# Layer 0's neighbour sum as seven products of half blocks in a two-layer graph kernel

## The chip, the cores and the metric

The program runs on one core of one Trainium2 chip. The metric is the device time of one execution in microseconds. Before the change it is 1271.28 us, the median of three runs (1270.83 to 1271.75).

## What is computed

There are 16 graphs (a "batch" b below is one graph) of 1024 nodes with 256 features. Two layers follow each other, each with a residual and a layer norm. Cut to what matters:

```python
# layer 0 (adj is 0 or 1 in the data, symmetric, with ones on the diagonal)
e0    = leaky(einsum('bid,bjd->bij', h * a0[:, 0], h))       # leaky: x or 0.2 x
alpha = sigmoid(where(adj == 1, e0, -max))
x     = layernorm(x + einsum('bij,bjd->bid', alpha, x) + bias)
# layer 1
Hh    = einsum('bni,io->bno', x, W)
s, d  = Hh @ a[:256], Hh @ a[256:]
e     = where(adj != 0, exp(-leaky(s[:, :, None] + d[:, None, :])), 0)
x     = layernorm(x + elu(einsum('bnm,bmo->bno', e, Hh) / e.sum(-1)))
```

All of it is fp32. A second, general pass for adjacency values other than 0 and 1 stands behind a flag and does not run with these inputs.

## The kernel before, in words

A batch has 1024 rows, eight tiles of 128. Everything is unrolled; the order of each engine's instructions is the order in which the code emits them (a manual schedule), and a scheduler adds the semaphores. An instruction that waits holds up all that stands behind it on its engine or queue. One turn of the loop over b (L572) has three stages and mixes three batches: layer 0 of b, layer 1 of b - 1 (`prev`) and the output of b - 2 (`done`).

**Strips** (L580 to L601). The matrix alpha is symmetric but for the mask, so only its upper triangle is computed. `strip(b, jt)` (L219) multiplies row tile jt with all columns from jt on: TensorE makes chunks of at most 512 columns in `ps_e` (three PSUM buffers), ACT takes two tanh of each (L241, L242), DVE their maximum (L243). `finish` (L245) adds one and multiplies by the adjacency (L249, DVE), and POOL adds twice the identity on the diagonal block (L259), which is the residual: `als[b]` is twice what multiplies x. `dump` (L261) turns 32 x 32 blocks on DVE (L265) and writes them to DRAM, `gather` (L271) fetches them as the mirrored blocks below the diagonal, both on SP's DMA queue; `mask(b, t)` (L277, L280, DVE) applies the adjacency to column tile t below the diagonal. In between, `project(prev, t)` (L397) multiplies the normed rows of b - 1, features on partitions in `x1T`, with W and the two vectors (TensorE, L411), and ACT takes exponentials (L419 to L421). `share_p` (L423) spreads one of the vectors over all partitions through DRAM on POOL's queue.

**Layer 0's sum** (L608 to L626). For each of eight row tiles t, `sum0` (L337) multiplies all eight blocks of column t with x: 8 x 8 products of 128 x 128 by 256 columns, each a pair of MATMUL records (L348), into a PSUM bank of `ps_acc` (three buffers). `end0` (L356) halves and adds the bias (L358, DVE, from PSUM) and takes the norm's statistics (`stats`, L299); after four tiles POOL computes the inverse roots (`center`, L321) and ACT scales the rows (`scale0`, L331). Beside this DVE does masks 3 to 6 and `weights(prev, m)` (L454, L460), ACT the scaling of b - 2's output and `check_adj` (L124). The normed rows go to DRAM (`save_x1`, L372) and come back in 32 x 32 blocks (`fetch_x1`, L380), which DVE turns (`turn_x1`, L385, L387): that is `x1T` for the next turn's projections.

**Layer 1's sum** (L631 to L671). For each row tile `sum1` (L464, L465) multiplies eight blocks of e with 257 columns; `elu` (L473) and `add` (L500) follow on DVE and ACT. Here x of b + 1, loaded in blocks, is turned and scaled (`turn_x`, L193: DVE, then ACT into `xa`), which the next strips need. SP carries `load_x`, `load_blocks` and the stores of the output; POOL's queue carries the adjacency (`load_adj`, L96, int32 to bf16).

Batch 0 has a start of its own (L525 to L570), the last batch an end of its own.

Of the kernel before, what the change touches and what calls it, by code (L numbers as in the profile page):

```python
# [18 lines left out]
P = 128  # L19
# [11 lines left out]
def one_kind_pass(  # L31
# [57 lines left out]
    def load_x(b, queues):  # L89
        xs[b] = two.tile([P, NT, D], F32, tag="x", name=f"x_{b}")  # L90
        rows = x[b].rearrange("(t p) d -> p t d", p=P)
        n = NT // len(queues)
        for g, queue in enumerate(queues):
            queue.dma_start(xs[b][:, ts(g, n), :], rows[:, ts(g, n), :])
# [43 lines left out]
    arow = two.tile([P, D], F32, tag="h", name="arow")[0:ND, 0:P]  # L138
    nc.scalar.dma_start(arow, a0.rearrange("(c p) o -> c (p o)", p=P))
# [23 lines left out]
    load_x(1, [nc.gpsimd])  # L163
# [4 lines left out]
    pcol = ps_e.tile([P, HALF], F32, tag="e", name="pcol")[:, 0:ND]  # L168
    nc.tensor.transpose(pcol, arow, ident[0:ND, 0:ND])
    nc.scalar.copy(acol, pcol)  # L170
# [5 lines left out]
    def make_Wx(c):  # L176

        for s in range(2):
            wprod = two.tile([P, D], F32, tag="h", name=f"wprod_{c}_{s}")
            nc.vector.tensor_tensor(wprod, Wx[:, c, 2:], a_bc[:, ts(s, D)], ALU.mult)  # L180
            nc.vector.tensor_reduce(Wx[:, c, s : s + 1], wprod, AX.X, ALU.add)

# [123 lines left out]
    def rstd(mv, what):  # L306
# [3 lines left out]
        nc.gpsimd.tensor_scalar(ve, mv[:, :, 1], EPS, None, ALU.add)  # L310
# [10 lines left out]
    def center(mv, what):  # L321

        r = rstd(mv, what)
# [3 lines left out]
        nc.gpsimd.tensor_scalar(mr, mr, -1.0, None, ALU.mult)  # L327
        return [(r[:, t : t + 1], mr[:, t : t + 1]) for t in range(n)]
# [4 lines left out]
    x1s, mv0s, r0s = {}, {}, {}  # L333
# [3 lines left out]
    def sum0(b, t):  # L337
        multiply0(b, t)
        end0(b, t)

    def multiply0(b, t):
        if t == 0:
            x1s[b] = two.tile([P, NT, D], F32, tag="x1", name=f"x1_{b}")
            mv0s[b] = small.tile([P, NT, 2], F32, tag="mv0", name=f"mv0_{b}")
            r0s[b] = []
# [10 lines left out]
    def end0(b, t):  # L356
        y = x1s[b][:, t, :]
        nc.vector.scalar_tensor_tensor(y, accs[t], 0.5, bias_bc, ALU.mult, ALU.add)  # L358
        stats(y, mv0s[b][:, t, :], f"0_{b}_{t}")
        if t % HT == HT - 1:  # L360
            g = t // HT
            r0s[b] += center(mv0s[b][:, ts(g, HT), :], f"0_{b}_{g}")
# [3 lines left out]


    x1Ts, Hs, pqs, p_bcs, es = {}, {}, {}, {}, {}

    x1_rows = {}  # L370
# [26 lines left out]
    def project(b, t):  # L397
# [21 lines left out]
        nc.scalar.activation(w, pt[:, 1:2], AF.Exp, scale=-SLOPE)  # L419
        nc.scalar.activation(pqs[b][:, :, t], pt[:, 0:2], AF.Exp, scale=SLOPE - 1.0)  # L420
        nc.scalar.mul(Hs[b][t][:, 0:D], pt[:, 2:], w)  # L421
# [108 lines left out]
    nc.sync.dma_start(bias_bc, bias.partition_broadcast(P))  # L530

# [12 lines left out]
    for t in range(NT):  # L544
# [12 lines left out]
        if t < 2:  # L557
            make_Wx(t)
        if t == 1:
# [4 lines left out]
        if t in (4, 5):  # L564
            scale0(0, 2 * t - 8)
            scale0(0, 2 * t - 7)
            turn_x(1, t - 4)
        if t == 5:
            save_x1(0, 0)
            fetch_x1(0, 0)  # L570

    for b in range(1, B):  # L572
# [4 lines left out]
        if prev == 0:  # L577

            projects = [[], [], [0, 1], [2, 3], [4, 5], [6, 7], [], []]
        for jt in range(NT):  # L580
            if jt == 4:
                mask(b, 0)
            strip(b, jt)
            if prev == 0 and jt < 2:
                scale0(0, HT + 2 * jt)
                scale0(0, HT + 2 * jt + 1)
# [5 lines left out]
            if prev == 0 and jt == 2:  # L592
                transpose_x1(0)
            if jt >= 1:
                gather(b, jt - 1)
            for t in projects[jt]:
                project(prev, t)
            if jt == 6:
                share_p(prev)
            if jt >= 6:  # L600
                mask(b, jt - 5)  # L601
        check_pq(prev)
        if not last:
            load_x(b + 1, [nc.sync])
# [3 lines left out]
        for t in range(NT):  # L608
            if 1 <= t < 5:
                mask(b, t + 2)  # L610
            for m in ([], [], [0, 1], [2], [3], [4], [5], [6, 7])[t]:
                weights(prev, m)
            if done >= 0:
                scale1(done, t)
                if t in (3, 7):
                    store(done, t - 3, HT)
            sum0(b, t)
            if t == 5 and not last:
                load_adj(b + 1, 0)
            if t in (5, 6):  # L620
                scale0(b, 2 * t - 10)
                scale0(b, 2 * t - 9)
            if t == 6:
                save_x1(b, 0)
            if t >= NT - CHECKS:
                check_adj(b, t - NT + CHECKS)  # L626
        if not last:
            load_adj(b + 1, 1)


        for t in range(NT):  # L631
# [3 lines left out]
            if last and t == 6:  # L635
                turn_x1(b, 1)
            if last and t == 3:
                turn_x1(b, 0)
# [9 lines left out]
            if t == 0:  # L648
                fetch_x1(b, 0)
            if t in (1, 2):  # L650
                scale0(b, 2 * t + 2)
                scale0(b, 2 * t + 3)
            if t == 2:
                save_x1(b, 1)
            if t == 4:
                fetch_x1(b, 1)
                if not last:
                    turn_x1(b, 0)
            if not last and t in (3, 5):
                turn_x(b + 1, (t - 3) // 2)  # L660
            if not last and t == 6:
                turn_x1(b, 1)
            if last and t in (4, 6):
# [3 lines left out]
                share_half(b, t0)  # L667
        if not last:
# [522 lines left out]
```

## Time and profile before

| what | value |
|---|---|
| median of three runs | 1271.28 us |
| span of the profiled execution, first to last instruction | 1268.6 us |
| around it (median less span) | 2.7 us |
| mean granted TensorE clock | 0.999 |
| L348, layer 0's products, 128x256 | 2048 records, 445.5 us busy |
| L465, layer 1's products, 128x257 | 2032 records, 444.9 us busy |
| DVE busy, all of the span | 925.2 us |
| DMA | 180.77 MB, 142 GB/s on average |

The execution time of the profiled run is not listed beside its span, so the median of the runs stands for it. PE is TensorE (matmul records), PEld its weight loads, DVE the vector engine, ACT the scalar engine, POOL GpSimd, SP the engine that issues most DMAs. In a group's line, "acc<-x,al" names what is written and read, xN the number of instructions, then the busy time, the mean in ns of one instruction, and the idle time ahead of them with what ended it. The mean of a matmul counts its time in the pipeline; what it costs in a row of others is read from the chain or from sums of busy time. In the timeline the first two columns are the start and the duration in us.

### The profile page before, as it was taken

The page shows a single profiled execution, that of the slowest core. Times are in us where ns is not written, and L with a number is a line of the kernel's source. Part 1 is how long each engine was busy: PE and PEld are TensorE (multiplying, and loading weights), DVE is VectorE, ACT ScalarE, POOL GpSimd, SP SyncE. Part 2 cuts the span into 40 slices and gives each one's busy share as a digit, 9 for nine tenths or more (in the row PEclk, how much of TensorE's full clock was granted, in tenths as well). Part 3 has the DMA queues.
Part 4 walks back from the last instruction along what each step waited for, and adds up shares of the span by engine and source line. Part 5 has one row for each costly group of instructions (what it writes and reads, how often), then busy time and mean ns, then how long its engine had stood idle before and what let it go on. Part 6 is the DMA issues. An engine that isn't in the chain of part 4 may idle for free.

```text
span 1268.6 us, 17528 instructions
## 1 busy us (share of the span) xinstructions
PE 1259.2 (99%) x5476; PEld 1024.5 (81%) x5476; DVE 925.2 (73%) x2027; ACT 650.2 (51%) x1467; POOL 299.7 (24%) x605
## 2 busy tenths in 40 slices
PE   9999999999999999999999999999999999999997
PEld 7788787887878878788787887878778787887886
DVE  5686867868678686876868868687686877858657
ACT  4645645456353564545645445454455644456434
POOL 2212231212312122121222212223122231212213
PEclk9999999999999999999999999999999999999999
DMA  9489595795959869497694966949579595895422
GB/s 213 80 171 155 92 197 92 168 185 106 190 90 177 168 124 198 78 174 159 131 203 83 184 131 139 210 80 190 113 167 185 97 192 95 171 183 99 109 51 69
DMA packets 603832, 180.77 MB, mean 142 GB/s; under 512 B 482010, under 2 KB 585940, under 8 KB 603732
## 3 DMA queue, kind: packets, MB, share of 16 engines
q1 hardware_dynamic: 581760, 135.85, 54.4%
q0 software_dynamic: 21280, 43.06, 18.7%
q8 instruction: 46, 0.75, 0.3%
q10 hardware_dynamic: 692, 0.66, 0.1%
q14 instruction: 54, 0.44, 0.1%
HBM read 152.44 MB, written 60.62 MB: 168 GB/s over the span
## 4 chain that ended last, share of the span: by engine, by line
PE 98%; DVE 1%; ACT 0%; issue 0%; ACTq 0%; DVEq 0%
PE acc L348 35%; PE acc L465 34%; PE pe L233 20%; PE pH L411 9%; PE busy L146 0%; PE pal L288 0%; PE pxT L209 0%; DVE st L301 0%; DVE y L505 0%; DVE y L503 0%; PE prow L427 0%; ACT y L331 0%; ACT y_kept L331 0%; ACT L680 0%; DVE mv L303 0%
## 5 line engine op out<-in xcount | busy, mean ns | idle before, releaser
L348 PE MATMUL acc<-x,al 128*128 128x256 f32 x2048 | 445.5, 379 | 0.0
L465 PE MATMUL acc<-H,e 128*128 128x257 f32 x2032 | 444.9, 379 | 0.0
L465 PEld LDWEIGHTS acc<-H,e 128*128 128x128 f32 x2032 | 384.9, 189 | 56.9
L348 PEld LDWEIGHTS acc<-x,al 128*128 128x128 f32 x2048 | 387.5, 190 | 51.8
L233 PE MATMUL pe<-xa,xT 128*128 128x384 f32 (+1 forms) x720 | 251.0, 486 | 0.0
L233 PEld LDWEIGHTS pe<-xa,xT 128*128 128x128 f32 x720 | 132.7, 189 | 80.9 <-issue 42.6
L331 ACT ACTIVATE x<-x,mr,r 128x256 f32<-128x256 f32 x128 | 69.4, 592 | 227.2 <-POOL mr L327 227.2
L460 DVE SCALAR_TENSOR_TENSOR e<-p,pq_kept,adj 128x1024 f32<-128x1024 f32 (+1 forms) x136 | 160.8, 1208 | 25.4 <-DMA p<-p_row 25.4
L310 POOL TENSOR_SCALAR ve<-mv 128x4 f32<-128x4 f32 (+2 forms) x49 | 16.2, 332 | 622.8 <-DVE mv L303 616.2
L497 ACT ACTIVATE h<-acc,rinv 128x256 f32<-128x256 f32 x126 | 59.1, 469 | 200.5 <-DVE rinv L489 185.1
L241 ACT ACTIVATE tb<-pe 128x512 f32<-128x512 f32 (+1 forms) x192 | 94.1, 490 | 120.3 <-PE pe L233 91.1
L488 DVE TENSOR_SCALAR rinv<-acc 128x1 f32<-128x1 f32 x127 | 19.9, 157 | 157.3 <-PE acc L465 156.8
L243 DVE TENSOR_TENSOR tb<-tb,low 128x512 f32<-128x512 f32 (+1 forms) x192 | 103.4, 544 | 38.6 <-ACT low L242 38.3
L128 ACT ACTIVATE junk<-adj,minus 128x2048 bf16<-128x2048 bf16 x64 | 127.3, 1989 | 0.0
L411 PE MATMUL pH<-Wx,x1T 128*128 128x258 f32 x512 | 126.3, 381 | 0.0
L411 PEld LDWEIGHTS pH<-Wx,x1T 128*128 128x128 f32 x512 | 97.2, 190 | 35.8 <-issue 14.3
L259 POOL TENSOR_TENSOR al<-ident,al 128x128 f32<-128x128 f32 x128 | 66.6, 520 | 227.2 <-DVE al L249 226.7
L249 DVE SCALAR_TENSOR_TENSOR al<-tb,adj 128x512 f32<-128x512 f32 (+7 forms) x132 | 97.5, 739 | 5.3 <-DVE tb L243 0.4
L242 ACT ACTIVATE low<-pe 128x512 f32<-128x512 f32 (+1 forms) x192 | 93.2, 485 | 0.5 <-DVE tb L243 0.5
L280 DVE SCALAR_TENSOR_TENSOR al<-al,adj 128x512 f32<-128x512 f32 (+3 forms) x150 | 76.1, 531 | 21.8 <-DMA al<-mir 21.7
L358 DVE SCALAR_TENSOR_TENSOR x<-acc,bias_bc 128x256 f32<-128x256 f32 x128 | 53.9, 421 | 41.5 <-PE acc L348 41.0
L265 DVE STREAM_TRANSPOSE tb<-tb 128x896 f32<-128x896 f32 (+6 forms) x105 | 74.7, 712 | 3.6
(110 smaller groups left out, 954.0 us busy)
## 6 DMA issues: line engine op xcount, KB each, us to landing
adj<-in_adjT POOLq DMA_DIRECT2D x30, 1024.0 KB, 10.3
x_rows<-x SPq DMA_DIRECT2D x31, 512.0 KB, 3.7
x1T<-x_rows SPq DMA_DIRECT2D x248, 64.0 KB, 2.6
out<-y_kept SPq DMA_DIRECT2D x30, 512.0 KB, 6.4
x<-in_x SPq DMA_DIRECT2D x14, 1024.0 KB, 6.0
xT<-in_x SPq DMA_DIRECT2D x112, 128.0 KB, 4.9
p<-p_row POOLq DMA_DIRECT2D x15, 512.0 KB, 4.5
mir<-tb SPq DMA_DIRECT2D x60, 112.0 KB, 3.0
```

What stands on the lines that cost most here:

```text
L128: nc.scalar.activation(junk, rows, AF.Square, bias=minus1, scale=2.0, accum_out=chk[:, b * CHECKS + n : b * CHECKS + n + 1],)
L233: nc.tensor.matmul(pe[:, 0:w], lhsT=xTs[b][:, c, ts(jt, P)], rhs=xas[b][:, c, ds(jt * P + o, w)], start=(c == 0), stop=(c == ND - 1),)
L241: nc.scalar.activation(tb[:, ds(o, w)], pe[:, 0:w], AF.Tanh, scale=0.5)
L242: nc.scalar.activation(low[:, 0:w], pe[:, 0:w], AF.Tanh, scale=0.5 * SLOPE)
L243: nc.vector.tensor_tensor(tb[:, ds(o, w)], tb[:, ds(o, w)], low[:, 0:w], ALU.max)
L249: nc.vector.scalar_tensor_tensor(als[b][:, jt, c0:c1], tbs[b, jt][:, c0 - jt * P : c1 - jt * P], 1.0, adjs[b, jt // HT][:, jt % HT, c0:c1] ...
L265: nc.vector.transpose(tb, tb)
L280: nc.vector.scalar_tensor_tensor(v, v, 1.0, rows, ALU.add, ALU.mult)
L348: nc.tensor.matmul(acc, lhsT=als[b][:, jt, ts(t, P)], rhs=xs[b][:, jt, :], start=(jt == 0), stop=(jt == NT - 1),)
L411: nc.tensor.matmul(pt, lhsT=x1Ts[b][:, c, ts(t, P)], rhs=Wx[:, c, :], start=(c == 0), stop=(c == ND - 1),)
L460: nc.vector.scalar_tensor_tensor(e, p_bcs[b][:, cols], q, rows, ALU.mult, ALU.min)
L465: nc.tensor.matmul(acc, lhsT=es[b][:, m, ts(t, P)], rhs=Hs[b][m], start=(m == 0), stop=(m == NT - 1),)
```

## The change

For b from 1 on, layer 0's sum is computed by Strassen's scheme (in Winograd's form) on half blocks: `als[b]` is cut in 2 x 2 blocks of 512 x 512, x in 2 x 2 blocks of 512 rows by 128 features. Seven products (`product`) of four steps each, x's blocks as weights and 512 columns of alpha moving, give y with features on partitions (`yT`), in four PSUM banks. The sums of blocks that they need are made by `combine_x` (POOL, in the strip stage, partly in x's place) and `combine_al` (in al's place: T1 and T4 on POOL, T2 on DVE, T3 half and half); `unite` puts the products together on ACT and DVE. Products 1 and 5 stand ahead of strip 6 on TensorE, the other five behind the strips. Masks 1 to 3 stand earlier than before.

`yT` is used by the projections as it is: norm 0's mean is taken out of W once (`center_Wx`), its root multiplies behind the product, on ACT (`rcols`). The rows of y, for the statistics and the residual, are made from `yT` by DVE (`turn_y`), written to DRAM in 32 x 32 blocks, and fetched (`fetch_y`); the statistics follow in layer 1's stage, `scale0` in the next turn. x has one buffer instead of two, and its load stands behind `fetch_y(b, 0)` on SP. Batch 0 keeps the old products. y is kept at twice its size, so epsilon and bias are scaled.

```diff
-        xs[b] = two.tile([P, NT, D], F32, tag="x", name=f"x_{b}")
+        xs[b] = one.tile([P, NT, D], F32, tag="x", name=f"x_{b}")
...
+    bcol = const.tile([P, ND], F32, tag="bcol", name="bcol")
+    nc.scalar.mul(bcol, pcol[:, ND:], 2.0)
...
+    def center_Wx():
+        mean_w = two.tile([P, HALF], F32, tag="low", name="mean_w")[:, 0:P]
+        nc.vector.memset(mean_w, 1.0 / D)
+        pw = ps_t.tile([P, HT, P], F32, tag="t", name="pw").rearrange("p t q -> p (t q)")[:, 0 : D + 2]
+        for c in range(ND):
+            nc.tensor.matmul(pw, lhsT=mean_w, rhs=Wx[:, c, :], start=(c == 0), stop=(c == ND - 1))
+        for c in range(ND):
+            nc.vector.tensor_tensor(Wx[:, c, :], Wx[:, c, :], pw, ALU.subtract)
...
-        y = x1s[b][:, t, :]
-        nc.vector.scalar_tensor_tensor(y, accs[t], 0.5, bias_bc, ALU.mult, ALU.add)
-        stats(y, mv0s[b][:, t, :], f"0_{b}_{t}")
+        nc.vector.tensor_tensor(x1s[b][:, t, :], accs[t], bias_bc, ALU.add)
+        stats0(b, t)
         if t % HT == HT - 1:
-            g = t // HT
-            r0s[b] += center(mv0s[b][:, ts(g, HT), :], f"0_{b}_{g}")
+            roots0(b, t // HT)
+    def stats0(b, t):
+        stats(x1s[b][:, t, :], mv0s[b][:, t, :], f"0_{b}_{t}")
+    def roots0(b, g):
+        r0s[b] += center(mv0s[b][:, ts(g, HT), :], f"0_{b}_{g}", 4.0 * EPS)
+        for k, f in enumerate((1.0, -SLOPE, SLOPE - 1.0)):
+            nc.gpsimd.tensor_scalar(
+                rcols[b][:, k, ts(g, HT)], r_all[f"0_{b}_{g}"], f, None, ALU.mult
+            )
...
+    Ss, yTs, Zs, banks = {}, {}, {}, {}
+    def combine_x(b, n):
+        x_, q = xs[b], (slice(0, P), slice(P, D))
+        if n == 0:
+            Ss[b] = one.tile([P, 3, HT, P], F32, tag="S", name=f"S_{b}")
+        s1, s2, s4 = (Ss[b][:, k, :, :] for k in range(3))
+        top, low = (x_[:, 0:HT, :], x_[:, HT:, :])
+        out_, in0, in1, op = (
+            (s1, top[:, :, q[1]], low[:, :, q[1]], ALU.add),
+            (s2, s1, top[:, :, q[0]], ALU.subtract),
+            (top[:, :, q[1]], top[:, :, q[0]], top[:, :, q[1]], ALU.subtract),
+            (s4, low[:, :, q[0]], s2, ALU.subtract),
+        )[n]
+        nc.gpsimd.tensor_tensor(out_, in0, in1, op)
+    def combine_al(engine, b, k, jt):
+        left, right = slice(0, HALF), slice(HALF, N)
+        top, low = als[b][:, jt, :], als[b][:, HT + jt, :]
+        t1, m12, m21, m22 = top[:, left], top[:, right], low[:, left], low[:, right]
+        out_, in0, in1 = {1: (t1, t1, m12), 2: (t1, m21, t1), 3: (m12, t1, m12), 4: (m21, m22, t1)}[k]
+        engine.tensor_tensor(out_, in0, in1, ALU.subtract)
+    def product(b, k):
+        left, right = slice(0, HALF), slice(HALF, N)
+        top, low = als[b][:, 0:HT, :], als[b][:, HT:, :]
+        x_ = xs[b]
+        lhs, rhs = {
+            1: (x_[:, 0:HT, 0:P], top[:, :, right]),
+            2: (x_[:, HT:, 0:P], low[:, :, right]),
+            3: (Ss[b][:, 2, :, :], low[:, :, left]),
+            4: (x_[:, HT:, P:D], low[:, :, left]),
+            5: (Ss[b][:, 0, :, :], top[:, :, left]),
+            6: (Ss[b][:, 1, :, :], top[:, :, left]),
+            7: (x_[:, 0:HT, P:D], top[:, :, right]),
+        }[k]
+        bank = {1: "Q", 2: "Q", 3: "V", 5: "V", 4: "W", 7: "W", 6: "R"}[k]
+        first = k in (1, 5, 6, 7)
+        if first:
+            pool, tag = (ps_acc, "acc") if bank in "QV" else (ps_e, "e")
+            banks[bank] = pool.tile([P, HALF], F32, tag=tag, name=f"p{bank}_{b}")
+        for jt in range(HT):
+            nc.tensor.matmul(
+                banks[bank],
+                lhsT=lhs[:, jt, :],
+                rhs=rhs[:, jt, :],
+                start=first and jt == 0,
+                stop=jt == HT - 1,
+                skip_group_check=True,
+            )
+    def unite(b, what):
+        yT = yTs[b]
+        left, right = slice(0, HALF), slice(HALF, N)
+        c12, c11 = yT[:, 0, left], yT[:, 0, right]
+        c22, c21 = yT[:, 1, left], yT[:, 1, right]
+        if what == "p1":
+            nc.scalar.copy(c12, banks["Q"])
+        elif what == "p5":
+            nc.scalar.copy(c22, banks["V"])
+        elif what == "u2":
+            nc.vector.tensor_tensor(c21, banks["R"], c12, ALU.add)
+        elif what == "c11":
+            nc.scalar.activation(c11, banks["Q"], AF.Identity, bias=bcol[:, 0:1])
+        else:
+            out_, acc, bias_, other = {
+                "s": (c22, banks["W"], bcol[:, 1:2], c22),
+                "c12": (c12, banks["V"], bcol[:, 0:1], c21),
+                "c21": (c21, banks["W"], bcol[:, 1:2], c21),
+                "c22": (c22, c22, None, c21),
+            }[what]
+            if bias_ is None:
+                nc.vector.tensor_tensor(out_, acc, other, ALU.add)
+            else:
+                nc.vector.scalar_tensor_tensor(out_, acc, bias_, other, ALU.add, ALU.add)
+    def new_yT(b):
+        yTs[b] = x1Ts[b] = one.tile([P, ND, N], F32, tag="x1T", name=f"yT_{b}")
+    def turn_y(b, c, g):
+        if b not in Zs:
+            Zs[b] = one.tile([P, ND, N], F32, tag="xa", name=f"Z_{b}")
+            y_rows[b] = dram.tile([N, D], F32, tag="x1_rows", name=f"y_rows_{b}")
+        half = ts(g, HALF)
+        nc.vector.transpose(Zs[b][:, c, half], yTs[b][:, c, half])
+        v = y_rows[b][half, :].rearrange("(nb a) (c q e) -> c q a nb e", a=SQ, c=ND, e=SQ)
+        for q in range(P // SQ):
+            nc.sync.dma_start(
+                v[c, q], Zs[b][ts(q, SQ), c, half].rearrange("p (nb e) -> p nb e", e=SQ)
+            )
+    def fetch_y(b, g):
+        if b not in x1s:
+            new_rows(b)
+        nc.sync.dma_start(
+            x1s[b][:, ts(g, HT), :],
+            y_rows[b].rearrange("(t p) d -> p t d", p=P)[:, ts(g, HT), :],
+        )
...
-        nc.scalar.activation(w, pt[:, 1:2], AF.Exp, scale=-SLOPE)
-        nc.scalar.activation(pqs[b][:, :, t], pt[:, 0:2], AF.Exp, scale=SLOPE - 1.0)
-        nc.scalar.mul(Hs[b][t][:, 0:D], pt[:, 2:], w)
+        r, r_s, r_p = (rcols[b][:, k, t : t + 1] for k in range(3))
+        wr = small.tile([P, 1], F32, tag="wr", name=f"wr_{b}_{t}")
+        nc.scalar.activation(w, pt[:, 1:2], AF.Exp, scale=r_s)
+        nc.scalar.mul(wr, w, r)
+        nc.scalar.activation(pqs[b][:, :, t], pt[:, 0:2], AF.Exp, scale=r_p)
+        nc.scalar.mul(Hs[b][t][:, 0:D], pt[:, 2:], wr)
...
+    load_x(1, [nc.sync])
...
+        masks = {4: [0], 5: [1], 6: [2]}
         for jt in range(NT):
-            if jt == 4:
-                mask(b, 0)
+            for t in masks.get(jt, []):
+                mask(b, t)
+                combine_al(nc.gpsimd, b, 1, t + 1)
+            if jt == NT - 2:
+                share_p(prev)
+                new_yT(b)
+                product(b, 1)
+                unite(b, "p1")
+                product(b, 5)
+                unite(b, "p5")
+            if jt == NT - 1:
+                mask(b, 3)
             strip(b, jt)
-            if prev == 0 and jt < 2:
-                scale0(0, HT + 2 * jt)
-                scale0(0, HT + 2 * jt + 1)
             finish(b, jt)
             if jt < NT - 1:
                 dump(b, jt)
             if prev == 0 and jt == 0:
                 turn_x1(0, 0)
-            if prev == 0 and jt == 2:
+            if prev == 0 and jt == 1:
                 transpose_x1(0)
             if jt >= 1:
                 gather(b, jt - 1)
+            if jt < 4:
+                combine_x(b, jt)
+            if jt == 3:
+                combine_al(nc.gpsimd, b, 1, 0)
             for t in projects[jt]:
                 project(prev, t)
-            if jt == 6:
-                share_p(prev)
-            if jt >= 6:
-                mask(b, jt - 5)
         check_pq(prev)
         if not last:
-            load_x(b + 1, [nc.sync])
             new_xT(b + 1)
             load_blocks(xTs[b + 1], x[b + 1], 0, N)
-        for t in range(NT):
-            if 1 <= t < 5:
-                mask(b, t + 2)
-            for m in ([], [], [0, 1], [2], [3], [4], [5], [6, 7])[t]:
-                weights(prev, m)
+        def extras(n):
+            if prev == 0 and n < 2:
+                scale0(0, HT + 2 * n)
+                scale0(0, HT + 2 * n + 1)
+            elif prev > 0:
+                scale0(prev, 2 * n)
+                scale0(prev, 2 * n + 1)
             if done >= 0:
-                scale1(done, t)
-                if t in (3, 7):
-                    store(done, t - 3, HT)
-            sum0(b, t)
-            if t == 5 and not last:
-                load_adj(b + 1, 0)
-            if t in (5, 6):
-                scale0(b, 2 * t - 10)
-                scale0(b, 2 * t - 9)
-            if t == 6:
-                save_x1(b, 0)
-            if t >= NT - CHECKS:
-                check_adj(b, t - NT + CHECKS)
+                for q in (2 * n, 2 * n + 1):
+                    scale1(done, q)
+                    if q in (3, 7):
+                        store(done, q - 3, HT)
+            check_adj(b, n)
+        for jt in range(HT):
+            combine_al(nc.vector, b, 2, jt)
+        product(b, 3)
+        for jt in range(HT):
+            combine_al(nc.vector if jt < 2 else nc.gpsimd, b, 3, jt)
+        extras(0)
+        product(b, 6)
+        weights(prev, 0)
+        mask(b, 4)
+        mask(b, 5)
+        weights(prev, 1)
+        mask(b, 6)
+        for jt in range(HT):
+            combine_al(nc.gpsimd, b, 4, jt)
+        unite(b, "u2")
+        extras(1)
+        product(b, 7)
+        weights(prev, 2)
+        weights(prev, 3)
+        unite(b, "c12")
+        extras(2)
+        product(b, 2)
+        unite(b, "s")
+        unite(b, "c22")
+        unite(b, "c11")
+        extras(3)
+        product(b, 4)
+        for m in range(4, NT):
+            weights(prev, m)
+        if not last:
+            load_adj(b + 1, 0)
+        for c in range(ND):
+            turn_y(b, c, 0)
+        fetch_y(b, 0)
+        unite(b, "c21")
         if not last:
             load_adj(b + 1, 1)
+            load_x(b + 1, [nc.sync])
         for t in range(NT):
             acc = acc1(prev, t, ps_acc, "acc")
             for m in range(NT):
                 sum1(prev, t, acc, m)
-            if last and t == 6:
-                turn_x1(b, 1)
-            if last and t == 3:
-                turn_x1(b, 0)
...
             if t >= 1:
                 add(prev, t - 1)
             if t == 0:
-                fetch_x1(b, 0)
+                for c in range(ND):
+                    turn_y(b, c, 1)
+                fetch_y(b, 1)
             if t in (1, 2):
-                scale0(b, 2 * t + 2)
-                scale0(b, 2 * t + 3)
-            if t == 2:
-                save_x1(b, 1)
-            if t == 4:
-                fetch_x1(b, 1)
-                if not last:
-                    turn_x1(b, 0)
-            if not last and t in (3, 5):
-                turn_x(b + 1, (t - 3) // 2)
-            if not last and t == 6:
-                turn_x1(b, 1)
+                stats0(b, 2 * t - 2)
+                stats0(b, 2 * t - 1)
+                if t == 2:
+                    roots0(b, 0)
+            if t in (3, 4):
+                stats0(b, 2 * t - 2)
+                stats0(b, 2 * t - 1)
+                if t == 4:
+                    roots0(b, 1)
+            if not last and t in (5, 6):
+                turn_x(b + 1, t - 5)
             if last and t in (4, 6):
                 t0 = (t - 4) // 2 * HT
                 for n in range(HT):
                     project(b, t0 + n)
                 share_half(b, t0)
+            if last and t in (5, 7):
+                for q in range(HT):
+                    scale0(b, (t - 5) // 2 * HT + q)
         if not last:
             add(prev, NT - 1)
             r1s[prev] = center(mv1s[prev], f"1_{prev}")
```

## The prediction

> **What bounds the kernel now.** I read the page first (busy shares, chain that ended last), then the chain in order of time for one batch in the middle, then busy time by stage, then single instructions where the change adds work.
>
> ```profile
> PE 1259.2 (99%) x5476; PEld 1024.5 (81%) x5476; DVE 925.2 (73%) x2027; ACT 650.2 (51%) x1467; POOL 299.7 (24%) x605
> ...
> PE 98%; DVE 1%; ACT 0%; issue 0%; ACTq 0%; DVEq 0%
> ...
> 600.53 3.43 PE pe L233 x8
> 623.10 27.63 PE acc L348 x128
> 650.73 27.84 PE acc L465 x128
> 678.57 3.43 PE pe L233 x8
> ```
>
> TensorE is the chain, without gaps, and a batch repeats after 678.57 - 600.53 = 78.04 us: 22.57 strips and projections, 27.63 layer 0's sum, 27.84 layer 1's. An fp32 product is two MATMUL records: 27.63/128 = 0.216 us per record of 256 columns, 3.43/8 = 0.429 per record of 512, so columns are what is paid. The stages' busy times (sum, then TensorE, weights, DVE, ACT, POOL) show who else is near:
>
> ```profile
> 600.50:623.10 22.60, 22.60 (x83) 14.89 (x82) 19.01 (x34) 15.92 (x48) 6.89 (x13) 1.00 0.57 102
> 623.10:650.70 27.60, 27.60 (x129) 24.29 (x129) 22.74 (x47) 12.39 (x22) 7.68 (x14) 1.00 0.97 185
> 650.70:678.60 27.90, 27.90 (x130) 24.30 (x129) 16.32 (x46) 12.25 (x23) 3.31 (x9) 1.00 0.76 151
> ```
>
> DVE is busy 19.0 of 22.6 and 22.7 of 27.6 us: only the last stage leaves it room.
>
> **What goes.** Per batch 64 products of 256 columns become 28 of 512: 56 x 0.429 = 24.02 against 27.63, so TensorE gives up **3.61 us a batch**, 54 us over 15 batches. DVE loses eight L358 (0.421) and two L387 (1.244), 5.9 us, and gains six combine_al and five unite steps (0.685 each, the row of 128x512) and four turn_y (0.712, L265 of that width), 10.4 us. Everything below is what this 3.6 us must pay. I follow one batch, t = 0 at its first strip (678.57 in the trace).
>
> **Added on POOL, and what it does to DVE.** Fourteen two-input adds of 512 elements: four combine_x, and combine_al's four of T1, two of T3, four of T4. None is in the trace. Nearest rows: POOL's 128x128 add 0.46 us unhindered and its 128x4 steps 0.20; the slope makes (0.46 - 0.20)/124 x 384 + 0.46 = 1.26 us (bounds: 0.46 if length were free, 4 x 0.46 = 1.84). Whether they run beside DVE is decided by these rows:
>
> ```profile
> 686.66 0.96 POOL L259 TENSOR_TENSOR al<-ident,al 128x128 f32<-128x128 f32 x1
> 689.45 0.45 POOL L259 TENSOR_TENSOR al<-ident,al 128x128 f32<-128x128 f32 x1 [1.83 <-DVE al L249]
> ...
> 686.61 0.69 DVE L243 TENSOR_TENSOR tb<-tb,low 128x512 f32<-128x512 f32 x1 [0.31 <-ACT low L242]
> 689.41 0.98 DVE L265 STREAM_TRANSPOSE tb<-tb 128x768 f32<-128x768 f32 x1
> ...
> 624.64 0.46 POOL L259 TENSOR_TENSOR al<-ident,al 128x128 f32<-128x128 f32 x1 [0.82 <-DVE al L249]
> 624.83 1.15 DVE L280 SCALAR_TENSOR_TENSOR al<-al,adj 128x256 f32<-128x256 f32 x2
> ...
> 636.32 0.39 DVE L280 SCALAR_TENSOR_TENSOR al<-al,adj 128x256 f32<-128x256 f32 x1
> ```
>
> The POOL add takes 0.96 when a DVE operation with two SBUF inputs is under way (it ends 0.32 after that one) and 0.45 beside a transpose. The other way round, a 256-mask takes 0.39 alone, and its pair with a 512-mask (0.685) takes 1.15 when POOL is ahead. So the two take turns, instruction by instruction, and a POOL add that meets such DVE work costs DVE about 1.1 us (1.26 less some start-up).
>
> The Trainium skill says the same more sharply ("SBUF — State Buffer", section "SBUF: two separate sides"): the pair of ports is locked for the whole instruction, the loser blocks fully. That speaks against adds on POOL. By the page the sum stays as it is; no row here shows it for an add as long as these.
>
> If a long add let DVE through after all, the rival of late rows alone applies.
>
> **Strip stage, to product 5.** TensorE alone reaches product 1 at 21.1 and would end product 5 at 28. Product 5's last quarter needs T1's row 3, which POOL makes after mask 2.
>
> ```profile
> 701.63 0.41 DVE L243 TENSOR_TENSOR tb<-tb,low 128x256 f32<-128x256 f32 x1
> ```
>
> Before, DVE begins strip 6 there, at t = 23.1, with mask 0 behind it. Masks 1 and 2 move ahead (0.469 + 0.685 + 0.272 + 0.685 = 2.1): 25.2. Seven POOL adds go before; some lie beside transposes (0.45 to 1.1 us) and DVE's waits of 0.3 to 1.1 us, so I charge 0.8 each: 30.8. T1's row 3: +1.1. Two matmuls (0.86): **product 5 ends at 32.8**. Without the turns it is 28.6.
>
> **Product 5 to product 3.** Product 3 needs mask 3, which stands on DVE behind strip 6's maximum, finish and transpose, and strip 6 stands on TensorE behind product 5. So after product 5: strip 6 0.86, two tanh 0.86, then 0.42 + 0.43 + 0.31 + mask 0.685 and a semaphore = 3.6. TensorE has only strip 7 (0.43) for it: 2.4 us idle in any case. share_p also moves right behind project 7 and waits for ACT's exponentials, 0 to 0.6 us (inside that idle time); its second DMA holds POOL for about 3.2 us (45.2 us, 14 times in the waits), with the diagonals of strips 6 and 7 behind it, which nobody needs before product 2. Gathers 5 and 6 issue on SP 4 us behind DVE, as before, and land ahead of masks 5 and 6. **Product 3 at 36.4** (without turns 32.3).
>
> **Product 3 to product 4.** Product 4 adds to product 7's bank, so it waits for the DVE step "s". Ahead of it on DVE: strip 7's 0.57, check 0.5, T2 and T3 6 x 0.685, four weights of 1.27, masks 4 to 6 1.29, u2, c12 and s 3 x 0.685 = 13.6. Six POOL adds fall here; four meet DVE: +3.6. s ends at 53.6; TensorE's products 3, 6, 7, 2 would be done at 36.4 + 13.7 = 50.1. Stall 3.5; **product 4 ends at 57.0**. Without turns both come out at 46, and product 4 ends at 49.5. (Old end of the sum: 50.2.)
>
> **The rows of y.** Then DVE does c22, waits one POOL add, four weights: 1.0 + 0.685 + 5.08, so turn_y starts at 60.3. Rows go to DRAM and back on SP's queue, 2 x (8 stores of 64 KB, one 512 KB fetch), with load_x (1 MB, median 6.0) between the halves.
>
> ```profile
> 656.27 8.38 SPq L120 DMA_DIRECT2D x1T<-x_rows  x8
> 668.05 4.62 SPq L120 DMA_DIRECT2D x1T<-x_rows  x8
> ...
> x_rows<-x SPq DMA_DIRECT2D x31, 512.0 KB, 3.7
> x1T<-x_rows SPq DMA_DIRECT2D x248, 64.0 KB, 2.6
> ```
>
> Eight such pieces take 8.4 + 2.6 = 11.0 beside an adjacency load and 4.6 + 2.6 = 7.2 without; the loads run here too, so I take 9 for each half (bounds 7.2 and 13.2, the second behind load_x). First issue 61.0, landed 70, fetched (0.4 + 3.7) 74.1. stats0(0) stands in DVE's order at t = 1 and would be reached at 66: **8 us of DVE idle, with elu and add behind it**. DVE then has stats 1.22, elu + add 1.9, stats, elu + add: 80.3. Second half: issued 70.8, 9, 4.1: 83.9, again a wait. Behind it 1.22 + 1.9 + 1.22 + 1.9 + 1.25 + 1.9 + 1.25 = 10.6 ends with turn_x(b+1, 1) at 94.5, and ACT's product xa (1.15) follows. The next strip needs it 0.9 us after its start: it begins at **94.9**. TensorE's own end of layer 1's sum is 57.0 + 27.8 = 84.9, held up besides by the three accumulators that elu frees late.
>
> Rest: the unite steps read PSUM, and L358 (PSUM and SBUF) shows no turn-taking; ACT gains 1.9 + 1.4 us and is at 41 of 78. Wx's centring adds some 1.5 us once. DVE's eight stats stay.
>
> **The sum.** Period 94.9 - 78.0 = +16.9. From strip (1,0) to strip (15,0) are 14 periods: +236.6. Last batch: no load_x, no turn_x, but its projections (t = 4, 6) wait for norm 0's roots, which now come after the fetched rows: product 4 6.8 late, then about 5.7: +12.5. Start +1.5. Profiled span 1268.6 + 250.6 = 1519.2; the median of the runs, 1271.28, is 2.7 above that span, so **1522, say 1520 us**. Clock: the first matmuls (L146) took 433 ns against 273 for 128 columns later, so an idle TensorE runs at a lower rate.
>
> By the skill ("TensorE: Matmul & The Clock Gate", Part 1) an idle window of some 3.4 us halves the clock until a busy one has passed. An estimate from that page: up to 1.7 us per long gap, some 5 us a batch; no row of this trace shows it in mid-kernel.
>
> **Rivals.**
> - *One of the two costs only.* POOL turns, but the rows arrive beside other work: 57.0 + 27.8 + 1.1 = 85.9 a batch, 14 x 7.9 + 14 = 1395. Or rows late without turns: everything 8.4 earlier, 86.5: 1404. For: DVE had 11.6 us free in the third stage. Against: the stats stand in order at t = 1.
> - *Neither costs.* 49.5 + 27.8 + 1.1 = 78.4: 1271 + 5 + 6 = 1282 up to 1330. Product 3's 2.4 us and the late xa eat the saving.
> - *Faster.* TensorE's columns decide alone, product 3's wait remains: 78.04 - 3.61 + 2.4 = 76.8, 14 x -1.2 - 2 = 1252; with no wait at all 1217. It decides once DVE's list from strip 7 to s is under TensorE's 13.7 us and both fetches land before DVE reaches the stats. For: TensorE is 98% of the chain. Against: the list alone is 13.6 without one POOL turn.
> - *The products are not cheaper* (a record of 512 over 2 x 0.216): the 0.429 excludes it.
> - *Worse.* Gaps lower the clock or stores queue behind load_x: over 1590.
>
> **Chances.** Forecast (1450 to 1590) 0.58, one of two (1360 to 1450) 0.22, neither 0.09, faster 0.04, the same 0.02, over 1590 0.05. Range 1360 to 1590 holds 0.80. A change within 0.2% can't be told from none. Faster 0.04, same 0.02, slower 0.94.
>
> **What would show it.** TensorE idle before product 5's last quarter, product 3 and product 4; POOL's 512-adds near 1.3 us, longer in pairs with DVE's two-input steps; the waits table led by DVE st waiting for DMA x1<-y_rows; a period of some 95 us with strips starting behind xa. Wrong if DVE's masks and weights keep their times beside POOL, if the fetched rows land before stats0's turn, or if TensorE's chain stays unbroken.

## The result and the profile after

The changed kernel takes **1570.26 us** (median of four runs, 1566.1 to 1573.58) against 1271.18 (four runs, 1270.83 to 1271.75): **1.235 times as long, 95% interval 1.2331 to 1.237**. The profiled execution took 1570.29 us with a span of 1568.5 and a mean granted clock of 0.949. That is slower, inside the range and in the direction forecast; the forecast of 1520 is 50 us short of a change of 299.

Below, "after" is the changed kernel. Its page, busy shares and the chain that ended last:

```profile
PE 1310.9 (84%) x4400; PEld 849.1 (54%) x4400; DVE 1153.1 (74%) x2105; ACT 725.0 (46%) x1641; POOL 607.3 (39%) x911
...
DVE 49%; PE 22%; DMA 16%; SPq 6%; issue 4%; ACT 3%; POOL 1%; DVEq 0%; ACTq 0%
```

TensorE has 1076 records fewer and is busy 52 us more: its records are longer (below). It was 98% of the chain and is 22%; DVE, DMA and SP's queue hold 71%.

One batch in the middle (the first two records of its strip 0 begin at 543.70). Each row gives a stretch from start to end, its length, then busy time and count of TensorE, weight loads, DVE, ACT and POOL, then the granted clock, the DMA share and GB/s:

```profile
543.70:578.20 34.50, 29.31 (x90) 16.59 (x91) 29.43 (x41) 20.87 (x59) 19.77 (x24) 1.00 0.47 94
578.20:601.10 22.90, 17.73 (x42) 8.41 (x40) 20.50 (x26) 16.69 (x29) 12.08 (x10) 0.85 0.50 112
601.10:606.30 5.20, 5.20 (x9) 2.18 (x10) 5.20 (x5) 1.48 (x2) 0.00 (x0) 0.67 1.01 164
606.30:641.50 35.20, 30.23 (x130) 25.08 (x128) 17.96 (x60) 6.25 (x14) 7.28 (x23) 0.95 0.63 141
```

The rows are: strips to product 5; to the end of the wait for "s"; product 4; layer 1's sum. The batch takes 97.8 us. In the first three DVE is busy 55.1 of 62.6 us, waits inside its instructions counted. In the last it is busy half of 35.2 us, and TensorE's 128 products, 27.9 us in a row before, are spread over it in pieces. So the first 63 us are DVE's, and the rest is held up by something that is on no engine. The table of waits after (us in total, times, longest) names it:

```profile
DVE st L313 <- DMA x<-y_rows: 187.5, 30, 10.8
...
PE acc L595 <- ACT y_kept L628: 66.9, 27, 4.6
...
PEld pe L245 <- ACT xa L210: 54.5, 26, 2.7
PE pW L435 <- DVE yT L468: 51.8, 15, 4.0
...
PE pV L435 <- POOL al L413: 34.6, 25, 2.3
...
PE pV L435 <- DVE al L292: 31.2, 14, 2.5
```

They are, from the top: statistics waiting for the rows from DRAM, layer 1's sum for accumulators that elu frees late (elu stands behind those statistics on DVE), strips for xa, product 4 for "s", product 5 for T1, product 3 for mask 3. The first on DVE's timeline of that batch, once for each half of the rows:

```profile
623.52 0.43 DVE L313 BATCH_NORM_STATS2 st<-x 128x6 f32<-128x256 f32 x1 [8.22 <-DMA x<-y_rows]
...
633.48 0.43 DVE L313 BATCH_NORM_STATS2 st<-x 128x6 f32<-128x256 f32 x1 [4.33 <-DMA x<-y_rows]
```

**Theory**: two costs in series make the time. (A) POOL's adds take turns with DVE until product 4. (B) The statistics stand in DVE's order ahead of other work, and wait there for rows still on their way. **Rivals**: the products on half blocks cost more than they save (C); the loads that share queue and DMA engines with the rows, not the trip itself, are what is slow (D); it is the order of the products (E). The experiments are single executions, each beside a run of the kernel before (1271.1 to 1271.3 us).

### The profile page after: what moved, and what is told of

Read it like the earlier page. It is cut to its first block, busy times and chain, and to the rows that moved or that the text cites. A ratio compares the mean times of both kernels' runs of the same rounds, so it can differ in the third digit from the quotient of the medians.

```text
span 1568.5 us, 15935 instructions
## 1 busy us (share of the span) xinstructions
PE 1310.9 (84%) x4400; PEld 849.1 (54%) x4400; DVE 1153.1 (74%) x2105; ACT 725.0 (46%) x1641; POOL 607.3 (39%) x911
## 4 chain that ended last, share of the span: by engine, by line
DVE 49%; PE 22%; DMA 16%; SPq 6%; issue 4%; ACT 3%; POOL 1%; DVEq 0%; ACTq 0%
DVE e L590 8%; PE pe L245 8%; DMA x<-y_rows 7%; DVE tb L255 7%; DVE al L292 6%; DVE al L413 6%; SPq L482 5%; DMA y_rows<-Z 5%; PE acc L595 5%; PE pW L435 4%; DVE al L261 4%; DVE st L313 4%; DMA mir<-tb 3%; DVE xT L209 2%; PE pH L538 2%
## 5 line engine op out<-in xcount | busy, mean ns | idle before, releaser
L413 POOL TENSOR_TENSOR al<-al 128x512 f32<-128x512 f32 x150 | 242.9, 1634 | 74.7 <-DVE al L413 31.7
L255 DVE TENSOR_TENSOR tb<-tb,low 128x512 f32<-128x512 f32 (+1 forms) x192 | 169.2, 893 | 116.9 <-ACT low L254 116.4
L313 DVE BATCH_NORM_STATS2 st<-x 128x6 f32<-128x256 f32 x128 | 51.7, 404 | 187.8 <-DMA x<-y_rows 187.5
L435 PE MATMUL pV<-al,S 128*128 128x512 f32 x240 | 130.5, 675 | 68.3 <-POOL al L413 34.6
L435 PE MATMUL pW<-al,x 128*128 128x512 f32 x240 | 125.6, 673 | 51.8 <-DVE yT L468 51.8
L538 PE MATMUL pH<-Wx,yT 128*128 128x258 f32 x480 | 121.0, 386 | 4.1 <-ACT y_kept L628 4.1
L435 PEld LDWEIGHTS pV<-al,S 128*128 128x128 f32 x240 | 47.1, 209 | 138.7 <-issue 79.6
L435 PEld LDWEIGHTS pW<-al,x 128*128 128x128 f32 x240 | 50.3, 215 | 124.0 <-issue 120.0
L538 PEld LDWEIGHTS pH<-Wx,yT 128*128 128x128 f32 x480 | 92.9, 194 | 40.2 <-issue 11.2
L435 PE MATMUL pQ<-al,x 128*128 128x512 f32 x240 | 110.7, 599 | 2.4 <-DVE al L292 2.4
L261 DVE SCALAR_TENSOR_TENSOR al<-tb,adj 128x512 f32<-128x512 f32 (+7 forms) x132 | 97.4, 739 | 5.0
```

Source lines behind the costliest of these rows:

```text
L255: nc.vector.tensor_tensor(tb[:, ds(o, w)], tb[:, ds(o, w)], low[:, 0:w], ALU.max)
L261: nc.vector.scalar_tensor_tensor(als[b][:, jt, c0:c1], tbs[b, jt][:, c0 - jt * P : c1 - jt * P], 1.0, adjs[b, jt // HT][:, jt % HT, c0:c1] ...
L313: nc.vector.bn_stats(st, y)
L413: engine.tensor_tensor(out_, in0, in1, ALU.subtract)
L435: nc.tensor.matmul(banks[bank], lhsT=lhs[:, jt, :], rhs=rhs[:, jt, :], start=first and jt == 0, stop=jt == HT - 1, skip_group_check=True,)
L538: nc.tensor.matmul(pt, lhsT=x1Ts[b][:, c, ts(t, P)], rhs=Wx[:, c, :], start=(c == 0), stop=(c == ND - 1),)
```

## The experiments

**e1_other_rows: B away.** The statistics read the rows of the batch before, which are there, with the factors rescaled; the norms are thereby another batch's.

```diff
-        stats(x1s[b][:, t, :], mv0s[b][:, t, :], f"0_{b}_{t}")
+        rows = x1s[b - 1] if b > 0 else x1s[b]
+        stats(rows[:, t, :], mv0s[b][:, t, :], f"0_{b}_{t}")
```

> Norm 0's statistics are taken from the rows of batch b - 1, which already lie there, so DVE waits for no fetched row; the roots are scaled down so that the exponentials stay finite, and the output is another one. Stores, fetches and all adds stay. My theory (two costs in a row: the rows of y, then POOL and DVE in turns): DVE loses its waits of 8.2 and 4.3 us a batch, turn_x comes right behind TensorE's sum, the period falls from 97.8 to some 89 us, the time to 1440 (1420 to 1460). Rival one (only the POOL adds count, the waits are slack that DVE needs for nothing): over 1540. Rival two (the trip through DRAM is all of it): 1300 or less.

Measured: **1438.05 us**, 132 less.

**e2_no_pool_adds: A away.** The ten combine_al and four combine_x steps on POOL are left out, so products work on blocks not combined and y is not the sum.

```diff
-            3: (Ss[b][:, 2, :, :], low[:, :, left]),
+            3: (x_[:, HT:, 0:P], low[:, :, left]),
...
-                combine_al(nc.gpsimd, b, 1, t + 1)
...
-            if jt < 4:
-                combine_x(b, jt)
```

> All 14 adds of 512 elements that stand on POOL are left out (the products take the blocks as they are, so the output is another one); DVE keeps its six, the rows of y make their trip. My theory: product 5 ends near 29 us after the strips' start instead of 32.4, s comes near 47 instead of 55, everything behind it moves up by 7 to 8 us: time 1460 (1440 to 1485). DVE's masks, weights and maxima of 512 go back to 0.69 and 1.27 us. Rival one (adds on POOL cost nothing, they lie beside DVE): 1550 or more. Rival two (adds are all of it): 1300 or less.

Measured: **1449.04 us**, 121 less. The busy times of e2's page:

```profile
PE 1274.6 (88%) x4400; PEld 841.3 (58%) x4400; DVE 975.0 (67%) x2105; ACT 723.5 (50%) x1641; POOL 289.7 (20%) x701
```

DVE is busy 975 us instead of 1153 with the same 2105 instructions, so POOL's adds had lengthened them by 178 us. That is 178/210 = 0.85 us for each POOL add. Product 5 has no wait left; in the table of waits of e2 the rows wait as long as ever:

```profile
DVE st L313 <- DMA x<-y_rows: 189.8, 30, 9.6
```

**e3_neither: both away**, with the edits of e1 and e2 together.

> Both edits of the two runs before: no POOL adds, statistics from other rows. My theory: the two gains add up, period near 79 us, time 1300 (1275 to 1330): still not faster than before, since product 3's wait for mask 3 and the late xa eat the 3.6 us that TensorE saves. Rival (the seven products alone pay): under 1260. Rival (something third, such as the clock, holds the time): over 1380.

Measured: **1289.59 us**, 281 less. So A and B together carry all but 18 us of the loss. Taken away singly they give 132 + 121 = 253.

**e4_eight_products: Strassen undone, all else kept** (features on partitions, rows via DRAM). 64 records of 512 instead of 56, no adds, the banks emptied by ACT:

```diff
+                lhsT=xs[b][:, jt, ts(c, P)],
+                rhs=als[b][:, jt, ts(g, HALF)],
+                start=jt == 0,
+                stop=jt == NT - 1,
...
+        nc.scalar.activation(
+            yTs[b][:, c, ts(g, HALF)], banks[c, g], AF.Identity, bias=bcol[:, c : c + 1]
+        )
```

> Strassen alone undone: y with features on partitions as eight plain products (64 records of 512 columns, 27.5 us of TensorE), no combine_x, no combine_al, four bank reads on ACT; norm 0 behind the projections and the rows through DRAM stay. Same output. My theory: the rows' trip alone stays, period 84 to 87 us, time 1385 (1360 to 1420). Rival (the rows' trip costs nothing without the adds): 1275. Rival (Strassen's adds cost nothing): 1550 or more.

Measured: **1415.19 us**, 155 less than after, 30 more than I expected, within the range. Without one add of blocks the kernel is still 11% slower than before. The table of waits of e4 shows the rows' trip again:

```profile
DVE st L313 <- DMA x<-y_rows: 157.1, 30, 7.1
```

and TensorE's timeline of e4 what it does: behind the late statistics elu and add free an accumulator late, and layer 1's last row tiles wait for it.

```profile
579.28 6.79 PE L539 MATMUL acc<-H,e 128*128 128x257 f32 x16 [4.78 <-ACT y_kept L572]
```

Sixteen records take 6.79 us after that gap; sixteen of the same kind took 3.75 at the end of the kernel, before and after. So undoing Strassen's scheme alone brings back 155 us; the other 144 us of the loss belong to what is kept here.

**e5_loads_behind: rival D.** x of b + 1 is loaded behind the second fetch, the adjacency behind the norm's roots.

```diff
             load_adj(b + 1, 1)
-            load_x(b + 1, [nc.sync])
...
                 fetch_y(b, 1)
+                if not last:
+                    load_x(b + 1, [nc.sync])
...
                     roots0(b, 0)
+                    if not last:
+                        load_adj(b + 1, 0)
```

> The changed kernel with its loads moved: load_x behind fetch_y(b, 1) on SP, the two adjacency loads behind norm 0's roots on POOL. Nothing is left out. The term tested is what the prediction charged to other transfers: 9 us for eight stores where 7.2 was the row without them. My theory: the first fetch lands some 12 us after the first store's issue instead of 16.4, the second some 11 us later, DVE's two waits fall from 12.5 to some 6 us a batch, time 1475 (1450 to 1505). Rival (the trip is issue and landing alone, loads do not matter): over 1550. A late adjacency would show as strips that wait for it.

Measured: **1448.96 us**, 121 less, more than my range gave. SP's queue after (start and length of the issues):

```profile
607.11 10.40 SPq L482 DMA_DIRECT2D y_rows<-Z  x8
619.64 0.38 SPq L490 DMA_DIRECT2D x<-y_rows  x1
620.07 0.50 SPq L94 DMA_DIRECT2D x<-in_x  x1
620.61 7.45 SPq L482 DMA_DIRECT2D y_rows<-Z  x8
629.72 0.38 SPq L490 DMA_DIRECT2D x<-y_rows  x1
```

The same in e5:

```profile
568.04 4.13 SPq L482 DMA_DIRECT2D y_rows<-Z  x8
573.81 0.38 SPq L490 DMA_DIRECT2D x<-y_rows  x1
574.24 5.19 SPq L482 DMA_DIRECT2D y_rows<-Z  x8
581.12 0.38 SPq L490 DMA_DIRECT2D x<-y_rows  x1
581.55 0.50 SPq L94 DMA_DIRECT2D x<-in_x  x1
```

From first store to fetch 5.8 us instead of 12.5, then 6.9 instead of 9.1; in that batch the statistics wait 3.46 and 1.43 us instead of 8.22 and 4.33. D is right as a part of B: moving the neighbours' loads brings 121 us, nearly the 132 of e1, where nothing waits for the rows.

Other rows tell the two loads apart. In after, load_x is issued at 620.07, behind the first fetch, so only the adjacency loads lie beside the first half's stores. e10, below, moves load_x alone. Its SP queue:

```profile
597.66 9.25 SPq L482 DMA_DIRECT2D y_rows<-Z  x8
609.06 0.38 SPq L490 DMA_DIRECT2D x<-y_rows  x1
609.49 6.10 SPq L482 DMA_DIRECT2D y_rows<-Z  x8
617.74 0.38 SPq L490 DMA_DIRECT2D x<-y_rows  x1
618.21 0.45 SPq L94 DMA_DIRECT2D x<-in_x  x1
```

From first store to fetch, the means of 14 batches are 11.9 and 9.4 us in after, 11.8 and 7.5 in e10, 6.2 and 7.2 in e5; in after's last batch, which loads no adjacency, the first half takes 5.7. So the adjacency loads cost the first half nearly 6 us, and load_x the second some 2.

**e6_p5_behind: rival E.** Product 5 stands behind strip 7, so that mask 3's chain (strip 6, tanh, maximum, transpose) runs beside it.

```diff
-                product(b, 5)
-                unite(b, "p5")
...
         check_pq(prev)
+        product(b, 5)
+        unite(b, "p5")
```

> Product 5 and its copy moved behind strip 7, nothing else. DVE then has strips 6 and 7 and mask 3 done while TensorE does product 5, so product 3 follows it at once. My theory (the back and forth between TensorE and DVE, 3.6 us from product 5's end to product 3, lies on the path): T2 starts 4 to 5 us earlier, time 1510 (1490 to 1530). Rival (that time is hidden by DVE's list behind it): 1565 or more.

Measured: **1524.18 us**, 46 less, 3.1 us a batch. Product 3's wait, 2.0 to 2.5 us in after, shrinks to 0.7 in most batches. The order matters, but is no rival to A and B.

**e7_adds_on_dve: the 14 POOL adds moved to DVE**, in the same places of the code.

```diff
-        nc.gpsimd.tensor_tensor(out_, in0, in1, op)
+        nc.vector.tensor_tensor(out_, in0, in1, op)
...
-                combine_al(nc.gpsimd, b, 1, t + 1)
+                combine_al(nc.vector, b, 1, t + 1)
```

> The 14 adds of POOL moved to DVE, same order of the code. DVE gets 14 x 0.685 = 9.6 us more of its own and loses the turns. My theory (a POOL add costs DVE about 0.7 us in the strip stage and 1.0 behind it, so DVE doing them itself is no dearer): 1530 (1505 to 1560), less than the changed kernel though POOL is empty. Rival (POOL does take work off DVE): 1600 or more.

Measured: **1495.0 us**, 75 less; I had expected 40, and it lies below my range. The busy times of e7's page:

```profile
PE 1304.5 (87%) x4400; PEld 851.6 (57%) x4400; DVE 1091.3 (73%) x2315; ACT 723.4 (48%) x1641; POOL 280.1 (19%) x701
```

and T2 and T3 in e7 on DVE's timeline:

```profile
556.21 4.89 DVE L413 TENSOR_TENSOR al<-al 128x512 f32<-128x512 f32 x8
```

DVE has 210 instructions more and is busy 62 us *less*. Eight such adds in a row cost it 4.89/8 = 0.61 us each, less than the 0.85 that each POOL add cost DVE by e2. An add "given away" to POOL was dearer for DVE than doing it. By the whole span, e7 against e2, an add on DVE cost (1091.3 - 975.0)/210 = 0.55 us.

**e8_neither_mended: can TensorE's saving be had at all?** e3 (so with the same parts left out) with product 5 behind strip 7, load_x behind the second fetch and both turn_x at t = 5.

> The run without POOL's adds and with statistics from other rows (wrong output for both reasons), and three orders mended: product 5 behind strip 7, both turn_x at t = 5, load_x behind fetch_y(b, 1). Left of the change are TensorE's seven products and DVE's six adds. My theory: product 3's wait of 2.4 and the strips' wait for xa of 0.9 us go, period near 75.5 against 78.0 before, time 1237 (1215 to 1255), faster than before: TensorE's saving is real and was eaten by the rest. Rival (longer records or the clock cost TensorE what it saves): 1271 or more.

Measured: **1254.12 us**, 17 faster than the kernel before, a batch every 76.45 us against 78.04. So C falls: the seven products do save TensorE's time, and the strips no longer wait for xa. Of the 3.61 us a batch 1.6 arrive; waits of 0.7 to 0.8 us for the shared row and for ACT's copy take part of the rest.

**e9_mended: the whole kernel with the cures together**: adds on DVE except combine_x, product 5 behind, load_x behind, statistics later (t = 3, 4, 6, 7), turn_x together, weights 1 to 3 moved towards "s" and behind it. The adjacency loads, which e5 moved too, stay where after has them.

```diff
-                combine_al(nc.gpsimd, b, 1, t + 1)
+                combine_al(nc.vector, b, 1, t + 1)
...
+            at = {1: 0, 2: 2, 3: 4, 4: 6} if last else {3: 0, 4: 2, 6: 4, 7: 6}
...
+            if not last and t == 5:
+                turn_x(b + 1, 0)
+                turn_x(b + 1, 1)
```

> A version with nothing left out, from what the runs showed: T's adds on DVE (combine_x stays on POOL), product 5 behind strip 7, load_x behind fetch_y(b, 1), both turn_x at t = 5, the statistics of the fetched rows at t = 3, 4, 6, 7 instead of 1 to 4, weights 2 and 3 behind s. My theory: the gains of the single runs (75 for the adds, 46 for product 5, 121 for the loads) add up but for TensorE's floor, period 78 to 80, time 1295 (1270 to 1325): level with the kernel before or a little over, since DVE has some 72 us of work in a batch. Rival (the gains overlap): over 1350.

Measured: **1339.75 us**, above the range. My sum counted all 121 us of e5, though the adjacency loads stay: the first half's stores still take 13.3 us to the fetch (mean of 14), and the statistics wait 77.5 us in total for rows, although they stand later. It may also have had too little for DVE, which is busy 83% of the span. Work put behind "s" has to be done before turn_x; TensorE's timeline of e9 shows the strips waiting for xa, and slow records behind the gap (5.67 us for eight, 3.6 in a row):

```profile
633.58 5.67 PE L245 MATMUL pe<-xa,xT 128*128 128x512 f32 x8 [1.85 <-ACT xa L210]
```

**e10_mended_weights_first: e9 with the weights and masks in the places of after.**

> The same, but the weights keep their place ahead of s. Product 4 then waits longer for s, layer 1's sum less for its weights. My theory: DVE's work from strip 7 to the last weight is the bound, so the place of the weights moves little: within 15 us of the other run, 1280 to 1330. Rival (product 4's wait alone counts): 25 us or more slower than the other.

Measured: **1325.56 us**, 14 less than e9, 245 less than after and 54 more than before. The single gains of e5, e6 and e7 are 121 + 46 + 75 = 242; that this is so near 245 is luck, since e10 lacks a part of e5 and of e7 and has other moves besides. What is left, from e10's chain:

```profile
PE 47%; DVE 36%; issue 9%; DMA 4%; ACT 1%; SPq 1%; POOL 1%; DVEq 0%; ACTq 0%; POOLq 0%
```

and from TensorE's timeline of e10:

```profile
591.56 5.40 PE L435 MATMUL pW<-al,x 128*128 128x512 f32 x8 [2.52 <-DVE yT L468]
```

DVE is busy 84% of the span, and product 4 still waits for its list. No version that computes the whole beat the kernel before. One with the adjacency loads moved as well was not run; e10's statistics wait 26.5 us in total for rows, about half of the 54.

## Why the prediction held, and where it was off

Own steps, in us from the start of strip 0. The effective start of the batch above is 545.73: the six records of strip 0 that stay together begin at 546.59, less 0.86 for the two that ran ahead and waited.

| step | predicted | measured |
|---|---|---|
| mask 2 done | 30.8 | 30.3 |
| product 5 ends | 32.8 | 32.4 |
| product 3 starts | 36.4 | 36.8 |
| "s" done | 53.6 | 55.2 |
| product 4 ends | 57.0 | 60.6 |
| turn_y starts | 60.3 | 60.6 |
| first half fetched, DVE goes on | 74.1 | 77.8 |
| second half fetched, DVE goes on | 83.9 | 87.8 |
| turn_x(b + 1, 1) ends | 94.5 | 97.4 |
| period | 94.9 | 97.9 (mean of 14) |

- **POOL's 512-add: right.** Estimated 1.26 us; 1.26 measured where nothing is in the way. **That it takes turns with DVE: right, and as hard as feared.** The trace of before showed it for adds of 0.46 us only. Here is a 384-maximum, mean 0.535 before, on DVE's timeline after:

```profile
555.12 1.57 DVE L255 TENSOR_TENSOR tb<-tb,low 128x384 f32<-128x384 f32 x1 [0.38 <-ACT low L254]
```

  and the POOL add beside it:

```profile
555.02 1.26 POOL L405 TENSOR_TENSOR S<-x 128x512 f32<-128x512 f32 x1
```

  It began 0.10 us after the POOL add and ended 0.41 after it: it stood still until POOL was done. The mean of DVE's 512-maximum and mask rose from 0.683 to 0.947 and from 0.685 to 0.967. This agrees with the Trainium skill ("SBUF — State Buffer", section "SBUF: two separate sides"), which has the shared ports locked for the whole instruction.
- **Product 3's back-and-forth through strip 6: right** (3.6 predicted, 4.4 measured from product 5's end); e6 takes it away and gets 46 us.
- **DVE's list from strip 7 to "s": mis-sized by 1.6 us.** I charged four of six POOL adds with 1.1 us. It did not reach turn_y, which starts at 60.6 against 60.3: I had DVE wait for a POOL add behind "s", and none was under way there. Two misses cancel; that is luck.
- **Product 4: the sum left the clock out.** I gave it 3.4 us. In the batch above it took 5.37, in a stretch at a granted clock of 0.67; it was slow (5.3 to 6.8) in nine of the 15 batches and took 3.67 in six. By the order of the code this costs after little, because turn_y stands behind DVE's weights, not behind product 4; no run shows it. In e1, where TensorE carries on at once, both misses show: the rival "POOL turns only" was 1395, e1 measured 1438. Its batches with a slow product 4 last about 89.2 us, the others about 88.0, so by estimate the clock is some 10 of these 43 us. Most of the rest is "s": product 4 waits for it until 56.0 to 56.7 us after strip 0 began, where I had 53.6.
- **The rows' trip: the largest error, a term of the right kind and too small.** I took 9 us for the eight stores of each half, between a row with (11.0) and one without (7.2) an adjacency load beside it. The second half, behind load_x, took 9.1; the first, beside two adjacency loads, 12.5. First half: 16.4 from first issue to DVE's going on, predicted 13.1, and these 3.3 are about what the period is off. The row of 11.0, with the load beside it, was the nearer one. It goes for e2 too (12.9 and 9.3 from first store to fetch, means of 14), which at 1449 lies 45 above the rival "rows late only" (1404).
- **The rival "neither" (1282 to 1330) holds**: e3 is 1290. **"Faster" holds under its two conditions**: 1252 was worked out, e8 measured 1254. That the numbers agree so closely is partly luck: 1252 kept product 3's wait of 2.4 us, which e8 has taken away, and e8 has other waits in its place.

The sum by its terms: 14 periods +277.4 (predicted 236.6), last batch +15.6 (12.5), start +6.9 (1.5); together 299.9 of span against 250.6. The start is a small step that was wrong in kind: W's centring has 3.5 us of idle TensorE ahead of it, in the middle of batch 0's products, and the sixteen records behind it take 5.06 instead of 3.62. TensorE's timeline after, near the start:

```profile
38.58 1.40 PE L191 MATMUL pw<-Wx,mean_w 128*128 128x258 f32 x4 [3.50 <-issue]
39.77 5.06 PE L363 MATMUL acc<-x,al 128*128 128x256 f32 x16
```

What stays open: what the clock alone costs in after (no run kept TensorE busy in the gaps), and how near the kernel before a whole version with the adjacency loads moved as well would come.

## What to carry to other kernels

Before work is taken off the engine that bounds a kernel, add up what the exchange gives to the engines beside it: here 3.6 us a batch of TensorE's time were paid with two-input adds that took DVE's time wherever they ran, and an add on POOL cost DVE more than the same add on DVE. A result sent through DRAM whose reader stands early in an in-order engine's list can cost that engine the rest of the trip, here 12.5 us of DVE's time in the batch shown, and the trip is as long as the loads beside it make it; put the reader as late as the work allows and other loads behind it. Price a step by the row taken under the nearest load, not by the middle of two.

## What the hardware showed beyond that

**Short gaps lower TensorE's clock, but not always.** Eight records of 512 took 3.6 us in a row. In e2 product 3 waits 2.40 us in every batch, and the gap ahead of that one lies 11 us back. Its eight records take 5.3 to 5.4 us in nine batches and 3.67 in six. TensorE's timeline of e2, one of each kind:

```profile
451.41 3.67 PE L435 MATMUL pV<-al,x 128*128 128x512 f32 x8 [2.40 <-DVE al L292]
...
631.34 5.37 PE L435 MATMUL pV<-al,x 128*128 128x512 f32 x8 [2.40 <-DVE al L292]
```

In after, the granted clock was 1.00 where such a product took 3.67 us (95.5 to 99.0) and 0.68 where it took 5.37 (192.6 to 197.9), both behind a gap of 2.40. So the length of the gap does not decide. The Trainium skill ("TensorE: Matmul & The Clock Gate", Part 1) has the clock judged over free-running windows of some 3.4 us; that fits a result that depends on where the gap lies. The gaps of 1.8 to 2.5 us that were followed by slow records are shorter than one such window, so a limit on the single gap would have missed them. An estimate by that page was 5 us a batch; no run here isolates it.
